# A graph network kernel on one core: a second block of 308 edge columns is sorted by source block and takes its rows from X in SBUF by one-hot products

## The chip, the cores and the metric

The kernel runs on one core of a Trainium2 chip. The metric is the device time of one execution in microseconds. Before the change its median is 8972.53 us over 11 runs, which lie between 8945.65 and 8996.13 us. Engines are named as in the profile: PE multiplies matrices (PEld loads its weights), DVE, ACT and POOL do elementwise work, SP issues transfers, and POOL also issues the indirect transfers that gather or scatter rows by an index.

## The reference, cut to what matters

Four graph layers run over one graph of 12500 nodes with 32 features and 400000 edges, which come sorted by destination. Each is followed by a residual sum and a layer norm. The change concerns the third layer, which runs a small network on every edge and takes the largest value at each destination.

```python
src = jax.random.randint(..., (400000,), 0, 12500)
dst = (12500 * jax.random.uniform(..., (400000,)) ** 2.0)   # then edges are sorted by dst
...
x = _layernorm(x + _L0_gnn_ref(x, src, dst, ...))           # attention over the edges
x = _layernorm(x + _L1_gnn_ref(x, edge_index, 3))           # 3 rounds of neighbour means
x = _layernorm(x + _L2_gnn_ref(x, edge_index, edge_attr_32, ...))
x = _layernorm(x + _L3_gnn_ref(x, edge_index))              # 3 rounds, normalised by degrees

def _L2_gnn_ref(x, edge_index, edge_attr, W1, b1, W2, b2):
    rol, col = (edge_index[0], edge_index[1])
    e_feat = jnp.concatenate([x[rol], x[col], edge_attr], axis=-1)
    h = jax.nn.relu(e_feat @ W1 + b1)
    v = h @ W2 + b2
    x_cand = jax.ops.segment_max(v, col, num_segments=num_nodes)
    return jnp.maximum(x_cand, x[:, -v.shape[-1]:])
```

Because destinations are squared uniforms, many edges share the low destinations.

## The kernel before

**Nodes and edges.** X lies in SBUF as 98 blocks (`H`) of 128 nodes by 32 features. Edges are taken as 3125 columns of 128.

**Stages.** First a matrix A of edge counts is built in DRAM while the attention layer uses it. Then come the three rounds of the second layer (`Rounds.product`, line 370), each a product of X with A. A round walks 25 chunks of 512 destinations; a chunk loads A in two halves (line 352) and runs 98 matmuls for each of its four quarters. Then the edge layer runs, and the three rounds of the fourth layer end the kernel; part of the first of those three is computed inside the edge layer (`round_part`, line 1354), the rest by `product` from block `HS[-1]` on.

**Side work in the second layer's rounds.** `sort_heavy` takes the first 308 columns (`HC`), whose destinations are all below 128, and sorts them by source block into 98 buckets of 512 rows (`sorted_d`). It is cut into steps by generators, and `product` takes a step twice a chunk, 51 in a round. `rank` works in round 0: 28 pieces, each a compare, a scan and a multiply on DVE (lines 606 to 612), four matmuls with `pick` (line 616) and a copy on ACT. `send` works in rounds 1 and 2: each of its 77 steps writes four positions on DVE (line 648) and issues four indirect scatters on POOL (line 116), one for each column; for every 22 columns `rows` loads edge attributes and copies them with two key columns into a row buffer on POOL (lines 636 to 640). Round 2 also scatters 98 blocks of X into `starts_d`, on the same POOL queue. In rounds 1 and 2 DVE also gathers bits of A's tiles (lines 380 to 387).

**The edge layer.** The other 2817 columns are worked in groups of four, in batches of 48 columns (`T`), in three stages of 1984, 512 and 321 columns (cuts by `HS`). For each column POOL issues one gather of source rows from `table` in DRAM (line 111). PE turns the four columns (line 1739), DVE copies the result out of PSUM (`eT`, line 1741), and behind that copy the indices `ids` of the group four ahead are written (line 1717), so gathers run four groups ahead. `hidden` (lines 1770, 1772) and `outer` (line 1788) are the edge network. Per batch DVE runs 64 scans: 32 spread each destination's row over its edges, 32 take running maxima. One stage's results are fetched with gathers when it ends (`done`), and then `round_part` of that stage fills the next.

**The sorted edges in the edge layer.** `heavy` works one bucket of 512 sorted edges as one part, 98 parts in all. Source rows come from a product of `X[:, b, :]` with a one-hot matrix, destination rows from `X[:, 0, :]` with another. A part has 12 steps; `fill` takes two steps at its first call in each group and one at its second, three a group, so 98 parts take 1177 steps or 392 groups, all of them in the first stage. Parts follow each other without overlap, since each holds the one buffer `z` in PSUM from its second step on. After the parts end, groups carry edges alone until a stage has ended.

```python
        def fill(i):
            for _ in range(2 - i):
                next(first[0], None)
            if fillers:
                k = 8 if fillers[0] in begun else 40
```

Tile orders the instructions of each engine when the program is built; the order on each engine is then fixed.

Of the kernel before, what the change touches and what calls it, by code (L numbers as in the profile page):

```python
# [22 lines left out]
P = 128  # L23
D = 32
# [36 lines left out]
HS = (52, 78)  # L61
# [59 lines left out]
def dense_path(ctx, tc, bad_i, x, src, dst, edge_attr, w1T, w1_b, w2, w2T, w2_b, aT,  # L121
# [23 lines left out]
    HE = P * HC  # L145
    ROW = D + 2
    scan = dram.tile([E - HE, D], F32, name="scan")
    sorted_d = dram.tile([H * SLOTS, ROW], F32, name="sorted_d")
# [65 lines left out]
    cuts = [HC]  # L214
# [333 lines left out]
    def sort_heavy(st):  # L548

        keep = st.enter_context(tc.tile_pool(name="h_keep", bufs=1))  # L550
        lo_f = keep.tile([P, HC], F32, name="lo_f")
        d1_f = keep.tile([P, HC], F32, name="d1_f")
        at = []
# [4 lines left out]
        n = HE // NR  # L558
        m = n // 4

        def rank():

            base = keep.tile([P, HC], F32, name="base")
            dsh = hk.tile([P, HC + 1], I32, name="dsh")
            nc.vector.memset(dsh[:, 0:1], -1)
            nc.gpsimd.dma_start(dsh[:, 1:], dst[:HE].rearrange("(p t) -> p t", p=P))
            nc.gpsimd.dma_start(dsh[1:, 0:1], bass.AP(tensor=dst.tensor, offset=dst.offset + HC - 1,
                                                      ap=[[HC, P - 1], [1, 1]]))
            hi = hk.tile([P, HC], I32, name="hi")
            nc.gpsimd.dma_start(hi, src[:HE].rearrange("(p t) -> p t", p=P))  # L570
            yield from range(2)
            nc.vector.tensor_tensor(lo_f, dsh[:, 1:], dsh[:, :HC], op=OP.is_lt)
            bad = hk.tile([P, 1], F32, name="bad")
            nc.vector.reduce_sum(bad, lo_f, axis=AX.X)
            nc.vector.tensor_add(more, more, bad)
            nc.vector.tensor_scalar(bad, dsh[:, HC:], float(P - 1), None, op0=OP.is_gt)
            nc.vector.tensor_add(more, more, bad)
            nc.vector.tensor_scalar(d1_f, dsh[:, 1:], 1.0, None, op0=OP.add)
            lo = hk.tile([P, HC], I32, name="lo")
            nc.vector.tensor_single_scalar(lo, hi, P - 1, op=OP.bitwise_and)  # L580
            nc.vector.tensor_copy(lo_f, lo)
# [3 lines left out]
            nc.scalar.dma_start(hi_d.rearrange("(p t) -> p t", p=P), hi8)  # L585
            nc.vector.tensor_scalar(base, hi, float(SLOTS), SLOTS / 2, op0=OP.mult, op1=OP.add)
            pick = hk.tile([P, 4, 4], BF16, name="pick")
            nc.vector.memset(pick, 0.0)
            for i in range(4):
                nc.vector.memset(pick[:, i, i:i + 1], 1.0)  # L590
# [4 lines left out]
            def load(c):  # L595
                t = hk.tile([P, n], U8, name="hib", bufs=2)
                nc.scalar.dma_start(t[:H], hi_d[None, c * n:(c + 1) * n].to_broadcast([H, n]))
                return t

            late = [load(0)]  # L600
            for c in range(NR):
# [18 lines left out]
                nc.scalar.dma_start(rank_d[c * n:(c + 1) * n].rearrange("(i t) -> i t", i=4), rk[:4])  # L620
            nc.vector.tensor_scalar(carry[:H], carry[:H], float(SLOTS), None, op0=OP.is_gt)
            nc.vector.tensor_add(more[:H], more[:H], carry[:H])
            to = keep.tile([P, HC], F32, name="at")
            nc.scalar.dma_start(to, rank_d.rearrange("(p t) -> p t", p=P))
            yield
            nc.vector.tensor_add(to, to, base)
            at.append(to)

        def send():

            k = HC // 14

            def rows(i):
                t = rp.tile([P, k, ROW], F32, name="hrow")
                u = rp.tile([P, k, D], F32, name="hattr", bufs=1)
                nc.gpsimd.dma_start(u, edge_attr[:HE].rearrange(
                    "(p t) d -> p t d", p=P)[:, i * k:(i + 1) * k, :])
                nc.gpsimd.tensor_copy(t[:, :, :D], u)
                nc.gpsimd.tensor_copy(t[:, :, D], lo_f[:, i * k:(i + 1) * k])
                nc.gpsimd.tensor_copy(t[:, :, D + 1], d1_f[:, i * k:(i + 1) * k])  # L640
                return t

            late = [rows(0)]
            for e in range(0, HC, 4):
                n = min(4, HC - e)
                pos = rp.tile([P, 4], I32, name="pos")[:, :n]
                with tc.issue_after(beats[-1].ins):
                    nc.vector.tensor_scalar(pos, at[0][:, e:e + n], 0.0, float(H * SLOTS - 1),
                                            op0=OP.max, op1=OP.min)
                for j in range(n):  # L650
                    i, u = divmod(e + j, k)
                    if u == 1 and i < 13:
                        late.append(rows(i + 1))
                    put = scatter(nc, sorted_d, pos[:, j:j + 1], late[i][:, u, :])
                    tc.declare_no_dep(put.ins, group="sorted", reason="one row for each edge")
                    tc.add_to_no_dep_group("sorted", put.ins)
                yield

        sent = send()
        return rank(), sent, sent  # L660
# [618 lines left out]
    nc.vector.memset(most, -BIG)  # L1279
    with ExitStack() as st:  # L1280
# [8 lines left out]
        def done(s):  # L1289
# [5 lines left out]
            def finish(h0, k, e):  # L1295
# [3 lines left out]
                if h0 == 0:  # L1299
                    nc.vector.tensor_max(e[:, 0, :], e[:, 0, :], most)  # L1300
                nc.vector.tensor_add(e, e, mb2[:, None, :].to_broadcast([P, k, D]))
# [65 lines left out]

        def fill(i):
            for _ in range(2 - i):
# [13 lines left out]
        def heavy(hidden, outer):  # L1383

            up = hw.tile([P, P], BF16, name="up")
            down = hw.tile([P, P], BF16, name="down")
            one = hw.tile([P, P], BF16, name="one")
            two = hw.tile([P, P], BF16, name="two")
            for t, at, v in ((up, -1.0, 1.0), (down, 1.0, 1.0), (one, 0.0, 1.0), (two, 0.0, 2.0)):
                nc.vector.tensor_scalar(t, jp, at, v, op0=OP.is_equal, op1=OP.mult)  # L1390
            next1 = hw.tile([P, 1], F32, name="next1")
            nc.vector.tensor_scalar_add(next1, place, 1.0)
            col1 = hw.tile([P, P], F32, name="col1")
            nc.gpsimd.iota(col1, pattern=[[1, P]], base=1, channel_multiplier=0,
                           allow_small_or_imprecise_dtypes=True)
            ends = [hw.tile([P, 4, D + 1], F32, name=f"ends{i}") for i in range(2)]
            for t in ends:
                nc.vector.memset(t[:, :, D:], 1.0)

            def load(b):  # L1400
                t = hw.tile([P, 4, ROW], F32, name="hrow", bufs=3)
                nc.scalar.dma_start(t.rearrange("p j d -> p (j d)"),
                                    sorted_d[b * SLOTS:(b + 1) * SLOTS].rearrange(
                                        "(p j) d -> p (j d)", p=P))
# [4 lines left out]

            late = [load(0), load(1)]  # L1410
            yield
            for b in range(H):
                if b + 2 < H:
                    late.append(load(b + 2))
                rw = late.pop(0)
                key = hw.tile([P, 2, 4], BF16, name="key", bufs=2)
                nc.vector.tensor_copy(key, rw[:, :, D:].rearrange("p j k -> p k j"))
                d1 = key[:, 1, :]
                yield
                z = psum.tile([P, CH], F32, name="z")  # L1420
                nc.tensor.matmul(z[:, 0:4], up, d1, start=True, stop=True)
                nc.tensor.matmul(z[:, 4:8], down, d1, start=True, stop=True)
                wide = []
                for m in range(2):
                    y = psum.tile([P, CH], F32, name="y", bufs=2)
                    for j in range(4):
                        nc.tensor.matmul(y[:, j * P:(j + 1) * P],
                                         key[:, m, j:j + 1].to_broadcast([P, P]), one,
                                         start=True, stop=True)
                    wide.append(y)  # L1430
                yield
                hot = hw.tile([P, 2, CH], F32, name="hot")
                nc.vector.tensor_scalar(hot[:, 0], wide[0], place, None, op0=OP.is_equal)
                nc.vector.tensor_scalar(hot[:, 1], wide[1], next1, None, op0=OP.is_equal)
                f = hw.tile([P, 2, 4], F32, name="f", bufs=2)
                kb = hw.tile([P, 4 * D], BF16, name="kb", bufs=2)
                nc.vector.tensor_tensor(f[:, 0], z[:, 4:8], d1, op=OP.is_equal)
# [3 lines left out]
                nc.vector.tensor_tensor(f[:, 1], z[:, 0:4], d1, op=OP.not_equal)  # L1441
                nc.vector.tensor_mul(f[:, 1], f[:, 1], d1)
                yield
                last = hw.tile([P, 4, P], F32, name="last", bufs=2)
                nc.vector.tensor_tensor(last, col1[:, None, :].to_broadcast([P, 4, P]),
# [4 lines left out]
                nc.tensor.matmul(pw[0:D], X[:, b, :], hot[:, 0], start=True, stop=True)  # L1450
                nc.tensor.matmul(pw[D:2 * D], X[:, 0, :], hot[:, 1], start=True, stop=True)
                for j in range(4):
                    nc.tensor.matmul(pT[2 * D:3 * D, j, :], rw[:, j, :D], ident, start=True,
                                     stop=True)
                nc.tensor.matmul(z[:, P:2 * P], kb, two,
                                 start=True, stop=True)
                yield
                eT = hw.tile([3 * D, 4, P], F32, name="heT")
                nc.scalar.copy(eT, pT[:3 * D])
                stay = hw.tile([P, P], F32, name="stay", bufs=2)  # L1460
                nc.scalar.copy(stay, z[:, P:2 * P])
                B = Part()
                B.v = hw.tile([P, 4, D], F32, name="hv", bufs=2)
                yield
                ready = hidden(B, eT)
                yield
                outer(ready)
                yield
                nc.tensor.transpose(z[:, 0:P], B.v.rearrange("p j d -> p (j d)"), ident)
                yield  # L1470
                o = hw.tile([P, P], F32, name="ho", bufs=2)
                nc.vector.tensor_tensor_scan(o, stay, z[:, 0:P], -BIG, OP.min, OP.max)
                yield
                nc.tensor.transpose(z[:, 2 * P:3 * P], o, ident)
                yield
                e = ends[b % 2]
                nc.scalar.copy(e[:, :, :D], z[:, 2 * P:3 * P].rearrange("p (j d) -> p j d", j=4))
                yield
                got = z[:, :4 * (D + 1)].rearrange("p (j d) -> p j d", j=4)
                for j in range(4):  # L1480
                    nc.tensor.matmul(got[:, j, :], last[:, j, :], e[:, j, :], start=True, stop=True)
                yield
                lack = hw.tile([P, 4], F32, name="lack", bufs=2)
# [973 lines left out]
```

## Time and profile before

| what | us |
|---|---|
| median of 11 runs | 8972.53 |
| profiled execution, own time | 8954.37 |
| its span, first to last instruction | 8952.5 |
| second layer, round 0 (1413 to 1900) | 487 |
| second layer, round 1 (1900 to 2490) | 590 |
| second layer, round 2 (2490 to 3130) | 640 |
| edge layer, with sorted parts (3180 to 5740) | 2560 |
| edge layer, edges alone (5740 to 6540) | 800 |
| a round of the fourth layer with no side work (8010 to 8470) | 460 |

A window's row tells the busy time of each engine in a stretch, with the count of its instructions in brackets, then the granted PE clock as a share of full speed, the busy share of the DMA engines and the GB/s moved. A wait's row tells who waited for whom, the sum in us, how often, and the longest. In a group's row the mean of one instruction stands after the busy time, and the idle time before it after the bar. Matmuls of a row overlap, so rows of PE do not add up to PE's busy time. Some matmul records are missing.

### The profile page before, as it was taken

How to read it: one execution, taken by the hardware profiler on the slowest of the kernel's cores; microseconds unless marked ns; L12 is line 12 of the kernel's file. 1: busy time of each engine (PE TensorE's matmuls, PEld its weight loads, DVE VectorE, ACT ScalarE, POOL GpSimd, SP SyncE). 2: the span in 40 equal slices, each digit the busy share in tenths (PEclk: the TensorE clock that was granted, in tenths of full speed). 3: DMA queues.
4: the chain of work that ended last, by engine and by line, in shares of the span. 5: the costliest groups of instructions: out<-in, count | busy, mean ns of one | idle time of the engine just before them, and what ended most of it. 6: DMA issues, size and time to landing. Idle time of an engine off the chain costs nothing. (4 is left out here: it accounts for less than half of the span.)

```text
span 8952.5 us, 194378 instructions
## 1 busy us (share of the span) xinstructions
PE 7030.8 (79%) x84402; PEld 5539.4 (62%) x84402; DVE 3929.0 (44%) x10962; ACT 1632.5 (18%) x3386; POOL 3568.8 (40%) x3459
## 2 busy tenths in 40 slices
PE   6788999998877967777777777656646885889998
PEld 4688998988877834444444444433323553579998
DVE  6999995524433534444444444333333223231111
ACT  1235882000000012112111112111111111100000
POOL 1005110025543155555555555666666556400000
PEclk7889999999988956666566665655557985999999
DMA  1156448988866821111111111111114652679998
GB/s 52 55 223 249 200 202 305 348 321 309 309 244 233 302 68 46 45 39 45 42 46 45 39 45 45 44 44 39 49 40 120 203 173 58 198 247 360 360 356 318
DMA packets 574722, 1447.42 MB, mean 162 GB/s; under 512 B 108407, under 2 KB 269791, under 8 KB 560415
## 3 DMA queue, kind: packets, MB, share of 16 engines
q1 hardware_dynamic: 433200, 1347.10, 41.2%
q0 software_dynamic: 109792, 66.25, 4.4%
q10 hardware_dynamic: 30864, 21.54, 0.9%
q8 instruction: 664, 10.88, 0.5%
q14 instruction: 202, 1.65, 0.1%
HBM read 1155.33 MB, written 279.27 MB: 160 GB/s over the span
## 5 line engine op out<-in xcount | busy, mean ns | idle before, releaser
L111 POOL DMA_INDIRECT ef<-table,ids x2817 | 2667.9, 947 | 1845.0 <-DVE ids L1717 879.7
L370 PE MATMUL y<-x,a 128*128 128x96 bf16 x49980 | 2339.6, 209 | 230.1 <-issue 206.6
L370 PEld LDWEIGHTS <-a 128*128 128x128 fp8e4 x49980 | 2241.3, 100 | 300.0 <-issue 271.4
L1788 PE MATMUL pv<-mw,hT 128*128 128x64 f32 x3208 | 764.0, 381 | 852.8 <-issue 388.7
L1788 PEld LDWEIGHTS pv<-mw,hT 128*128 128x128 f32 x3208 | 645.4, 280 | 1185.4 <-issue 572.5
L1741 DVE COPY eT<-pT 96x512 f32<-96x512 f32 x705 | 478.6, 679 | 1521.4 <-remote 595.5
L1770 PE MATMUL ph<-eT,mw 96*64 96x256 f32 x1410 | 681.3, 580 | 222.2 <-ACT hT L1775 89.2
L1007 PE MATMUL pa<-oh,ol 128*128 128x196 bf16 x4928 | 731.4, 272 | 128.6 <-DVE oh L997 82.0
L1739 PE MATMUL pT<-ident,ef 128*96 128x128 f32 x2817 | 729.1, 367 | 31.2 <-remote 22.9
L1013 ACT ACTIVATE at<-pa 128x784 uint16<-128x784 f32 x816 | 646.8, 824 | 506.9 <-PE pa L1007 477.8
L1775 ACT ACTIVATE hT<-ph,mb 128x256 f32<-128x256 f32 x802 | 380.8, 475 | 1730.0 <-PE ph L1772 607.9
L278 DVE TENSOR_REDUCE v<-y 128x128 f32<-128x384 f32 (+2 forms) x152 | 83.6, 550 | 1372.1 <-PE y L272 802.9
L1772 PE MATMUL ph<-eT,mw 96*64 96x256 f32 x1408 | 681.6, 581 | 0.2 <-issue 0.2
L1739 PEld LDWEIGHTS pT<-ident,ef 128*96 128x96 f32 x2817 | 428.0, 178 | 394.8 <-issue 309.1
L1043 PE MATMUL y<-x,at 128*128 128x102 bf16 x9604 | 639.4, 209 | 10.8 <-DVE x L258 6.3
L116 POOL DMA_INDIRECT sorted_d<-hrow,pos x308 | 410.0, 1331 | 590.9 <-DVE v L1237 221.6
L1007 PEld LDWEIGHTS <-ol 128*128 128x128 bf16 x4928 | 556.9, 149 | 142.8 <-issue 78.9
L997 DVE TENSOR_TENSOR oh<-bins_h,pl 128x1568 bf16<-128x1568 bf16 x616 | 597.3, 970 | 0.0
L1043 PEld LDWEIGHTS <-at 128*128 128x128 fp8e4 x9604 | 556.2, 98 | 24.0 <-issue 11.8
L111 POOL DMA_INDIRECT g<-code_d,ws_i x25 | 216.0, 8639 | 807.3 <-DVE ki L781 588.0
L1354 PE MATMUL y<-a,x 128*96 128x512 fp8e4 (+1 forms) x1950 | 516.2, 402 | 16.2 <-DMA a<-A 8.1
L992 DVE TENSOR_TENSOR ol<-la,lb 128x1024 bf16<-128x1024 bf16 x616 | 422.0, 687 | 64.4 <-PE pa L1007 63.3
(409 smaller groups left out, 7065.3 us busy)
## 6 DMA issues: line engine op xcount, KB each, us to landing
a<-A SPq DMA_DIRECT2D x245, 3136.0 KB
A<-at SPq DMA_DIRECT2D x98, 1568.0 KB
a<-A SPq DMA_DIRECT2D x144, 832.0 KB
ef<-table,ids POOLq DMA_INDIRECT x2817
starts_d<-rows SPq DMA_DIRECT2D x44, 1024.0 KB
attr<-in_edge_attr SPq DMA_DIRECT2D x57, 768.0 KB
begin<-starts_d SPq DMA_DIRECT2D x57, 768.0 KB
scan<-o SPq DMA_DIRECT2D x57, 768.0 KB
```

Source lines behind the costliest of these rows:

```text
L111: return nc.gpsimd.indirect_dma_start(out=o, out_offset=None, in_=tab, in_offset=IndirectOffsetOnAxis(ap=idx, axis=0))
L370: nc.tensor.matmul(y[:, q, :], block(h, q - q0), x3[:, h, :3 * F], start=(q + h == first), stop=(c >= CX and q == nq - 1 and h == H - 1))
L997: nc.vector.tensor_tensor(oh, bins_h[:, None].to_broadcast([P, 4, HJ, 2]), pairs(pl[:, t, 0, half * 64 + w0:half * 64 + w0 + 8])[:, :, Non ...
L1007: nc.tensor.matmul(pa[:, 2 * b + i, :HJ], ols[t][:, :, :, 4 * u + 2 * b + i].rearrange("p a b -> p (a b)"), ohs[t][:, 2 * u + b, :, i], st ...
L1013: nc.scalar.activation(at[:, qd, :, off:off + 8].rearrange("p h (w j) -> p h w j", w=4), pa[:, :, :HJ].rearrange("p w (h j) -> p h w j", h ...
L1043: nc.tensor.matmul(y[0][:, q, :], at[:, q - 2 * half, h, :], x3[:, h, :3 * F0], start=(q + h == 0), stop=(not EARLY <= c < CX and last and ...
L1354: nc.tensor.matmul(y[:3 * D, :nq * Q], x3[:, h, :3 * D], a[:, :nq, h - h0, :], start=(h == lo), stop=(h == hi - 1))
L1739: nc.tensor.transpose(pT[:3 * D, j, :], B.ef[:, t + j, :], ident)
L1741: behind = nc.vector.tensor_copy(eT[:, :k], pT[:3 * D, :k])
L1770: nc.tensor.matmul(ph[:HID, :ka], mw1, eT[:, :ka], start=True, stop=True)
L1772: nc.tensor.matmul(ph[HID:2 * HID, :k - 2], mw1, eT[:, 2:k], start=True, stop=True)
L1788: nc.tensor.matmul(pv[:, j].rearrange("p h d -> p (h d)"), hT[:, j, :], mw2, start=True, stop=True)
```

## The change

The columns 308 to 615, whose destinations must lie below 512, are ranked, sent and worked like the first 308. `sorted_d` doubles in buckets and gains a column for the destination block (its rows grow from 34 to 35 words). The edge layer keeps 2509 columns. `HS` moves from (52, 78) to (56, 82), so that its stages have 1764, 492 and 253 columns, and `T` from 48 to 44. In round 0 the two ranks run one after the other, two steps at a time. `send` has 88 steps of seven columns, and its row buffers hold 14 columns.

`heavy` now has 196 parts, of kind 0 (as before) and kind 1 by turns. A kind 1 part takes its four possible destination blocks at once: one product with `X[:, 0:4, :]`, from which a comparison with the block number selects (`sel`), a hidden layer in four matmuls with the weights split in two, and a last product that is 132 wide, for four blocks, instead of 33. A part is cut into `front` (6 steps for kind 0, 8 for kind 1) and `back` (5 steps); the back of one part is worked along with the front of the next. `fill` takes 7 steps in two groups instead of 6. The last products of all parts go into `most` (block 0) and `most4` (blocks 0 to 3).

```diff
-HS = (52, 78)
+HS = (56, 82)
...
+        def ranks():
+            for g in range(2):
+                steps = rank(g)
+                for _ in steps:
+                    next(steps, None)
+                    yield
...
-            k = HC // 14
+            k = 14
...
             late = [rows(0)]
-            for e in range(0, HC, 4):
+            for e in range(0, 2 * HC, 7):
...
-                for j in range(n):
+                for j in range(7):
...
         def fill(i):
-            for _ in range(2 - i):
+            turn.append(i)
+            for _ in range(1 if len(turn) % 4 == 0 else 2):
                 next(first[0], None)
...
+            def hidden4(B, eT, sel):
+                ph = psum.tile([P, 2, P], F32, name="ph")
+                for o, sl in ((ph[:HID], slice(0, 2)), (ph[HID:], slice(2, 4))):
+                    nc.tensor.matmul(o, w_sa, eT[:2 * D, sl], start=True, stop=False)
+                    nc.tensor.matmul(o, w_d, sel[:, sl], start=False, stop=True)
+                hT = hw.tile([P, 2, P], F32, name="hhT")
+                nc.scalar.activation(hT, ph, AF.Relu, bias=mb1)
+                return B, 0, 4, hT
...
+                if kind:
+                    y = psum.tile([P, CH], F32, name="y", bufs=2)
+                    nc.tensor.matmul(y, X[:, 0:NB, :].rearrange("p h d -> p (h d)"), hot[:, 1],
+                                     start=True, stop=True)
+                    yield
+                    sel = hw.tile([P, 4, P], F32, name="sel")
+                    nc.vector.scalar_tensor_tensor(sel.rearrange("p j e -> p (j e)"), wb, blk, y,
+                                                   op0=OP.is_equal, op1=OP.mult)
...
+                for j in range(4):
+                    nc.tensor.matmul((pT if j % 2 else z)[:, j // 2 * W4:(j // 2 + 1) * W4],
+                                     B.last[:, j, :],
+                                     e4[:, j].rearrange("p b d -> p (b d)"), start=True, stop=True)
...
+            for i in range(2 * H):
+                B = Part()
+                B.i, B.b, B.kind = i, i // 2, i % 2
+                for _ in front(B):
+                    next(prev, None)
+                    yield
+                for _ in prev:
+                    yield
+                prev = back(B)
...
-    T = 48
+    T = 44
```

## Prediction

> **What bounds the kernel now.** I read the slices first, then a table of windows by stage, then the waits and the timeline inside the stages that the change touches. The product rounds come first in time. In the table, the figures after each engine are its busy time and, in brackets, its instructions; the last three are granted PE clock, DMA share and GB/s.
>
> ```profile
> 1413.00:1900.00 487.00, 468.26 (x10263) 448.97 (x10264) 198.33 (x265) 26.74 (x77) 0.13 (x1) 0.99 0.96 353
> 1900.00:2490.00 590.00, 509.95 (x10311) 486.55 (x10308) 259.81 (x455) 15.43 (x52) 321.11 (x242) 0.92 0.82 304
> 2490.00:2880.00 390.00, 297.40 (x5252) 274.96 (x5250) 137.25 (x232) 3.31 (x15) 161.41 (x159) 0.82 0.61 225
> 2880.00:3130.00 250.00, 227.97 (x4826) 220.91 (x4823) 128.66 (x199) 2.46 (x12) 46.10 (x48) 0.94 0.83 309
> 8010.00:8470.00 460.00, 446.40 (x10176) 443.33 (x10175) 53.85 (x164) 14.92 (x50) 0.00 (x0) 0.99 0.96 363
> ```
>
> The reader is to see that a round without POOL work does 10176 matmuls in 460 us, 45.2 ns each, and that the same matmuls take longer as soon as POOL (fifth figure) scatters. At 45.2 ns the second, third and fourth windows would take 466, 237 and 218 us; they take 124, 153 and 32 us more. The same windows asked for the scatters alone hold 204, 148 and 48 of them: 0.61, 1.03 and 0.67 us lost for each. The timeline shows how:
>
> ```profile
> 2620.40 0.96 POOL L116 DMA_INDIRECT sorted_d<-hrow,pos  x1 [0.30 <-issue]
> ...
> 2621.66 0.96 POOL L116 DMA_INDIRECT starts_d<-X,start_i  x1 [0.30 <-issue]
> 2622.22 0.37 PE L370 MATMUL y<-x,a 128*128 128x96 bf16 x5 [1.04 <-issue]
> ...
> 2622.93 0.96 POOL L116 DMA_INDIRECT starts_d<-X,start_i  x1 [0.30 <-issue]
> ...
> 2623.67 0.41 PE L370 MATMUL y<-x,a 128*128 128x96 bf16 x3 [1.07 <-issue]
> ```
>
> While scatters follow each other every 1.26 us, PE does three to five matmuls and then stands for about 1 us, waiting for nothing that the profile shows.
>
> The edge layer is the other half:
>
> ```profile
> 3180.00:5740.00 2560.00, 1868.71 (x8574) 1153.87 (x8573) 1056.77 (x4155) 509.11 (x1320) 1466.97 (x1551) 0.60 0.18 43
> 5740.00:6540.00 800.00, 480.68 (x1667) 254.74 (x1667) 261.25 (x1041) 117.52 (x298) 508.44 (x538) 0.51 0.19 46
> 6780.00:7330.00 550.00, 458.40 (x2394) 271.22 (x2392) 173.73 (x693) 90.56 (x238) 323.49 (x342) 0.89 0.60 185
> ```
>
> and of the waits between 3100 and 5700 us, who waited for whom, sum, times, longest:
>
> ```profile
> POOL ef L111 <- DVE ids L1717: 561.5, 162, 8.3
> POOL ef L111 <- issue: 416.9, 1319, 2.2
> ```
>
> First the sorted parts run (1551 POOL instructions, nearly all gathers), then edges alone, then edges with the fourth layer's product. Four gathers, one group, take 2560/1551 x 4 = 6.60 us, 800/538 x 4 = 5.95 us and 550/342 x 4 = 6.43 us. POOL itself needs 4 x (0.95 + 0.30) = 5.0 us. The rest it waits for `ids`, which DVE writes behind the copy `eT`, which waits for PE. So PE's chain sets the pace, not POOL. A group costs PE 4.82, 3.57 and 5.36 us of busy time; times the granted clock (0.60, 0.51, 0.89) this is 2.89, 1.82 and 4.77 us of full-speed work, and PE stands idle 1.78, 2.38 and 1.07 us a group.
>
> **What is removed.** 2817 columns are 705 groups, 2509 are 628. The sorted parts take 1177/3 = 392 groups before; after, a pair takes 6 + 8 = 14 steps, 98 x 14 / 3.5 = 392 groups. So the 77 groups saved are ones without parts: 55 in the first stage (496 to 441) at 5.95 us, 327 us, and 22 in the later two at 6.43, 141 us. Against the 141 stand 100 more matmuls of `round_part` (82 rows for 78, 25 chunks) at 516.2/1950 = 0.265 us, 26 us, and a tail: the last stage has 64 groups, its product begins about 27 groups in and needs 26 x 25 / 16 = 41, so four groups' worth, 64 x 0.265 = 17 us, is left over. Together **-425**. Batches go from 60 to 59 and not to 53, since `T` shrinks: some 5.6 batches of 64 scans at 0.295 us, 106 us of DVE, are not saved. DVE is a third busy there, which hides most; without that cover all of it: 0 to 106, I take **+20**. The later rest of the fourth layer's first round starts from block 82 instead of 78: 400 of 2000 matmuls less in the 120 us from 7880, **-24**.
>
> **Round 0.** A second rank is 28 more pieces. On DVE 28 x 5.9 us (0.94 + 3.15 + 0.15 + 1.62) = 165 us more beside 198 busy of 487: hidden by the waits for PE, and if that cover failed PE would wait for the post-processing. On PE the four matmuls of line 616 took 22.7 us for 112, and PE has no room in this window. ACT copies and its transfers (28 loads and 28 stores more on ACT's queue, 27 us busy of 487) are off the path. 10 to 60, **+25**.
>
> **Rounds 1 and 2.** 308 more scatters, in 51 + 37 steps of seven, so 14 a chunk instead of 8. Queued behind them on POOL are the 98 scatters to `starts_d`; behind the wait for a free `pos` on DVE stand the reductions and with them the PSUM buffers of PE. Row loads go from 14 to 44. Ends: 0.61 us each, the cheapest row, where DVE's long bit operations hold POOL (a scatter then takes up to 7.85 us and PE does not stutter), 188 us; or POOL itself as the bound, 308 x 1.27 + 30 row loads x 4.5 us (copies 0.78 + 0.22 + 0.22, issue 0.58, wait 2.67) = 526. The densest window, 1.03, is nearest for both rounds, but about three of fourteen will fall under bit operations: 0.9 x 308 = **+277**.
>
> [...]
>
> **The sorted parts.** The first kind comes at the same rate (0.25 a group for 0.255). New is 0.25 of a kind 1 part. The trace gives kind 0 in full-speed PE work: (2.89 - 1.82)/0.255 = 4.2 us. Kind 1 by the rows, in busy us a part: kind 0 sums to 8.3 (wide 1.04; the three overlapping products and turns 2.35 in the timeline; 0.29; shifts 0.36; hidden 0.82; outer 0.95; turns 0.82; last 1.69). Kind 1 has 12 wide matmuls for 8 (1.56), one small product with the turns (1.9), a full one (1.9), 0.29, shifts in float32 twice 0.36, hidden twice 0.82, 0.95, 0.82, and the last one 132 wide, which the trace lacks: 1.69 if weights bound it, 6.8 if columns do, 8 x 0.38 = 3.06 by the 128-wide turn of line 1469. Sum 12.8, 1.54 times kind 0. Work a group: 1.82 + 0.25 x 4.2 x 2.54 = 4.5 us.
>
> What a group then takes is work over clock plus idle. Low end: as beside the fourth layer's product, whose work is 4.77: 6.43 us, -66 us over 392 groups. High end: clock and idle as now, 4.5/0.60 + 1.78 = 9.28, +1050. The product in the low row waits for nobody, while the parts chain PE to DVE and ACT through one `pv` and one `ph` in PSUM; yet busier PE was granted more clock in these rows. I take the middle of both, clock 0.75 and idle 1.42: 4.5/0.75 + 1.42 = 7.42, 0.82 x 392 = **+321**. DVE gets about 1.8 us a group more (two compares 1.48, `last` and `sel` 1.32, eight more at 0.28 to 0.74, a quarter of 7.3) on 2.72: 61% of 7.42, not the bound. ACT stays under 35%.
>
> [...]
>
> Zeroing grows by about 2 MB beside a build whose DMA share is 0.57 to 0.65 (600 to 1500 us): 0.
>
> **The sum.** -425 + 20 - 24 + 25 + 277 + 321 = +194. On the profiled execution's own 8954.4 us (span 8952.5 and 1.9 around it) that is 9148; it lies 18 below the median of the runs, so for the median 8972.5 + 194 = **9167**.
>
> **Rivals.**
> 1. *PE absorbs the second kind* (faster). Place: the groups with parts. The clock rises as beside the product and a group stays at 6.60: the 321 go, -127, **8845**. It decides below 6.60 + 127/392 = 6.92 us a group. For it: the product's window. Against: the kind there now already costs 0.65 us a group. 0.26.
> 2. *POOL becomes the bound of rounds 1 and 2.* The send takes 526 instead of 277: +443, **9415**. For it: `pos` already waits for scatters' landing; against: POOL is busy 321 of 590 us. 0.13.
> 3. *The clock stays at 0.60.* +1050 instead of 321: +923, **9895**. For it: 0.51 to 0.60 wherever PE waits for others; against: 0.89 at 83% busy. 0.09.
> 4. *It doesn't do what it says*: a bucket over 512 rows, or a destination over 511, sends the input down the general path. 39424/98 = 402 edges a bucket and 12500 x (78848/400000)^2 = 486 speak against: 0.01. Effects that cancel within 0.2%, about what this kernel's runs can tell from no change: 0.04.
>
> **How the numbers follow.** My forecast has 0.47, own range 8990 to 9400. Slower is 0.47 + 0.13 + 0.09 + 0.01 = 0.70, faster 0.26, same 0.04. The range 8800 to 9600 leaves out rival 3 and a third of rival 1, about 0.18.
>
> **What would show it.** Rounds 1 and 2 together near 1500 us for 1230, with more "issue" waits before line 370; POOL near full there if rival 2 holds. Groups with parts at 7.4 us, clock near 0.75; under 6.9 proves me wrong and rival 1 right. 2509 gathers; 5.95 us still where edges run alone. Round 0 near 510. I am wrong altogether if scatters in longer runs cost less than 0.6 us and groups stay at 6.6.

## The result, and the profile after

The changed kernel takes 9618.46 us (median of 8 runs, 9577.71 to 9641.01) against 8972.57 (31 runs): a ratio of 1.0714, interval 1.0698 to 1.073. It is slower, as forecast, but by 646 us where 194 were predicted, and 18 us outside the range of 8800 to 9600. The profiled execution, from which all stages below are read, took 9562.93 us; its span is 609 us longer than that of the kernel before.

The stages of the profiled execution, by the same windows as before (busy time and instructions of PE, PEld, DVE, ACT and POOL, then granted PE clock, DMA share, GB/s). First the three rounds of the second layer, then the edge layer with sorted parts, with edges alone, and with the fourth layer's product:

```profile
1475.00:2016.00 541.00, 459.10 (x9638) 423.57 (x9639) 344.69 (x368) 37.71 (x101) 0.13 (x1) 0.98 0.82 297
2016.00:2773.00 757.00, 569.25 (x10237) 519.79 (x10234) 256.61 (x433) 15.42 (x52) 493.89 (x484) 0.84 0.67 241
2773.00:3605.00 832.00, 597.44 (x10221) 541.27 (x10218) 276.69 (x456) 5.98 (x28) 421.35 (x436) 0.79 0.56 205
...
3633.00:6768.00 3135.00, 2526.26 (x13672) 1583.24 (x13673) 1668.36 (x6441) 785.13 (x2121) 1509.43 (x1572) 0.76 0.15 38
6790.00:7130.00 340.00, 169.44 (x668) 102.48 (x666) 115.64 (x494) 47.61 (x122) 214.94 (x229) 0.51 0.19 47
7560.00:8010.00 450.00, 399.38 (x2103) 238.12 (x2102) 152.04 (x652) 74.61 (x194) 265.64 (x281) 0.92 0.64 204
```

The fourth row is the largest loss: 392 groups in 3135 us are 8.00 us each, where 6.59 stood before. Edges alone still take 340/229 x 4 = 5.94 us. The copies `eT` and the reductions that end the blocks of a round give the stages of every kernel in the same way; the table below holds them. Round 0 is counted here from the end of its first block to that of its last (443 us before, where the prediction's window had 487), and rounds 1 and 2 from there. A group with parts is the mean of the first 392; "groups after" runs from copy 392 to the last copy (in brackets, how many), "tail" from there to the end. Each row is one profiled execution.

| kernel | round 0 | rounds 1+2 | us a group with parts | groups after | tail | span |
|---|---|---|---|---|---|---|
| before | 443 | 1235 | 6.59 | 2042 (313) | 1153 | 8952.5 |
| after | 541 | 1589 | 8.00 | 1585 (236) | 1207 | 9561.1 |
| b0, kernel before again | 445 | 964 | 5.00 | 1705 (313) | 1152 | 7715.4 |
| a0, changed kernel again | 541 | 1377 | 5.92 | 1299 (236) | 1222 | 8260.0 |
| e1 one block sent | 545 | 1122 | 5.96 | 1296 | 1211 | 8008.0 |
| e2 kind 1 idle | 542 | 1411 | 5.16 | 1305 | 1216 | 7991.8 |
| e3b ranks spread | 521 | 1382 | 5.94 | 1296 | 1215 | 8235.6 |
| e4 plain transfers | 541 | 1309 | 5.95 | 1298 | 1212 | 8185.1 |
| e5 more PE work | 544 | 1383 | 5.93 | 1304 | 1211 | 8258.5 |
| e6 more DVE work | 544 | 1376 | 7.42 | 1296 | 1216 | 8833.1 |
| e7 HS back | 541 | 1372 | 5.91 | 1302 | 1155 | 8180.3 |
| e8 gathers 8 ahead | 544 | 1387 | 5.98 | 1271 | 1245 | 8277.8 |
| e9 positions ahead | 550 | 1340 | 5.94 | 1300 | 1209 | 8215.1 |
| e10 e9, e3b, e7, e8 | 526 | 1396 | 5.89 | 1267 | 1188 | 8181.9 |
| e11 e9, start values ahead | 552 | 1086 | 5.96 | 1299 | 1214 | 7982.2 |
| e12 eT on ACT | 540 | 1377 | 5.42 | 1291 | 1210 | 8026.1 |
| e13 e11, e3b, e7, e12 | 525 | 1151 | 5.42 | 1303 | 1156 | 7746.1 |
| e17 e9, start values first | 550 | 967 | 5.91 | 1297 | 1222 | 7846.6 |
| e16 e17, e3b, e7, e12 | 527 | 968 | 5.43 | 1302 | 1166 | 7586.9 |
| e15 kernel before, eT on ACT | 441 | 962 | 5.00 | 1693 (313) | 1154 | 7698.3 |

All the experiments ran on five chips on which the kernel before takes 7707 to 7729 us, and not 8972; so they are compared with b0 and a0, the two kernels unchanged on one such chip, and not with the first two rows. Most experiments are a single execution; e13, e15 and e16 have 6, 10 and 5 runs. Stages that an edit does not touch differ by up to 34 us in rounds 1 and 2 (1411 in e2, 1377 in a0) and by under 0.1 us a group.

There the change costs 545 us of span for 609, and partly by other waits. Who waited for whom in rounds 1 and 2 (1904 to 3139, 2016 to 3605, 1908 to 2872 and 2016 to 3394 us), sum, times, longest. PE in the kernel before, then PE and DVE in the changed kernel, all in the first pair:

```profile
PE y L370 <- issue: 165.0, 318, 1.4
```

```profile
PE y L372 <- issue: 364.3, 633, 1.9
```

```profile
DVE pos L677 <- DMA sorted_d<-hrow,pos: 123.6, 16, 10.5
```

The same for PE in b0, then PE and DVE in a0:

```profile
PE y L370 <- issue: 45.4, 75, 2.0
```

```profile
PE y L274 <- DVE spread L267: 188.2, 19, 13.5
PE y L372 <- DMA a<-A: 137.6, 13, 19.8
...
PE y L372 <- issue: 13.7, 24, 1.2
```

```profile
DVE pos L677 <- DMA sorted_d<-hrow,pos: 747.2, 81, 12.7
```

So the stops without a wait that the prediction priced rose from 165.0 to 364.3 us in the first pair, and hardly occur in a0. What holds PE in a0 is named: DVE stands 747 us before the next seven positions, because the scatters that read the last but one set have not landed; the copies into `spread` (line 267) and the reading of A's tiles stand behind it on DVE, and PE waits for `spread` and for the next tiles of A.

### The profile page after: what moved, and what is told of

The parts are those of the page before. It is cut to its first block, busy times and chain, and to the rows that moved or that the text cites. A ratio compares the mean times of both kernels' runs of the same rounds, so it can differ in the third digit from the quotient of the medians.

```text
span 9561.1 us, 205071 instructions
## 1 busy us (share of the span) xinstructions
PE 7599.0 (79%) x88296; PEld 5923.8 (62%) x88296; DVE 4566.0 (48%) x12909; ACT 1850.2 (19%) x4039; POOL 3690.4 (39%) x3626
## 5 line engine op out<-in xcount | busy, mean ns | idle before, releaser
L111 POOL DMA_INDIRECT ef<-table,ids x2509 | 2400.7, 957 | 2193.7 <-DVE ids L1859 981.0
L372 PE MATMUL y<-x,a 128*128 128x96 bf16 x49588 | 2449.5, 212 | 415.4 <-issue 392.3
L372 PEld LDWEIGHTS <-a 128*128 128x128 fp8e4 x49588 | 2303.4, 101 | 538.8 <-issue 509.3
L116 POOL DMA_INDIRECT sorted_d<-hrow,pos x616 | 735.7, 1194 | 523.0 <-issue 185.8
L1930 PEld LDWEIGHTS pv<-mw,hT 128*128 128x128 f32 x2900 | 513.1, 248 | 664.4 <-issue 298.3
L1930 PE MATMUL pv<-mw,hT 128*128 128x64 f32 x2900 | 608.0, 345 | 316.4 <-ACT hT L1917 135.7
L1912 PE MATMUL ph<-eT,mw 96*64 96x256 f32 x1256 | 547.0, 528 | 205.9 <-DVE eT L1883 123.1
L1881 PE MATMUL pT<-ident,ef 128*96 128x128 f32 x2509 | 525.7, 335 | 37.5 <-remote 16.4
L1914 PE MATMUL ph<-eT,mw 96*64 96x256 f32 x1254 | 554.9, 535 | 0.1
L1529 PE MATMUL pT<-hot,X 128*32 128x512 f32 x392 | 319.6, 912 | 259.2 <-DVE hot L1508 256.6
L1881 PEld LDWEIGHTS pT<-ident,ef 128*96 128x96 f32 x2509 | 343.8, 157 | 239.2 <-issue 183.3
```

The source lines that it names most:

```text
L111: return nc.gpsimd.indirect_dma_start(out=o, out_offset=None, in_=tab, in_offset=IndirectOffsetOnAxis(ap=idx, axis=0))
L116: return nc.gpsimd.indirect_dma_start(out=tab, in_=i, in_offset=None, out_offset=IndirectOffsetOnAxis(ap=idx, axis=0))
L372: nc.tensor.matmul(y[:, q, :], block(h, q - q0), x3[:, h, :3 * F], start=(q + h == first), stop=(c >= CX and q == nq - 1 and h == H - 1))
L1881: nc.tensor.transpose(pT[:3 * D, j, :], B.ef[:, t + j, :], ident)
L1912: nc.tensor.matmul(ph[:HID, :ka], mw1, eT[:, :ka], start=True, stop=True)
L1914: nc.tensor.matmul(ph[HID:2 * HID, :k - 2], mw1, eT[:, 2:k], start=True, stop=True)
```

## The experiments

**The two kernels again (b0, a0).** No edit.

> The kernel before, unchanged, to have its stages in this chip's clock beside the others of this set. If this chip grants more PE clock than in the profile of before (the first four experiments had 5.95 us a group with both kinds of parts), then a group with parts takes 5.0 to 5.4 us for 6.59 and one without 4.9 to 5.2 for 5.95; if the clock is the old one, all stages are as they were within 2%.

> The changed kernel, unchanged, beside the kernel before in the same set. Theory: three terms carry the loss (scatters in rounds 1 and 2, the second kind's work, round 0), of which the scatters' does not depend on the granted clock: rounds 1 and 2 stay 150 us or more over before's, round 0 70 to 100 us over, groups with parts 0.6 us or more over. Rival: all of the loss comes from the low granted clock; then at a higher clock the kernels are within 2% of each other.

The windows with parts of b0 and of a0:

```profile
2897.00:4859.00 1962.00, 1628.59 (x8685) 1013.51 (x8685) 1062.81 (x4206) 510.68 (x1333) 1485.54 (x1565) 0.72 0.24 58
```

```profile
3417.00:5739.00 2322.00, 2046.43 (x13682) 1317.06 (x13683) 1654.40 (x6443) 785.42 (x2121) 1509.74 (x1574) 0.95 0.21 52
```

The rival is out: with more clock the loss stays, +96 in round 0, +413 in rounds 1 and 2, 0.92 us a group (+360). In b0 a group with parts takes 5.00 us, which is POOL's 4 x (0.95 + 0.30), a gather and the wait before the next (1485.54/1565 and 358.3/1176 us), and PE waits 280.8 us for gathered rows: there the gathers set the pace, and not PE's chain as in the profile that was read for the prediction.

**One block sent (e1), plain transfers (e4).**

```diff
-            for e in range(0, 2 * HC, 7):
+            for e in range(0, HC, 7):
```

> Leaves out the second block's row loads and 308 scatters (its buckets stay zero); all else is as in the changed kernel. Theory: rounds 1 and 2 grew from 587+649 to 774+834 us because of the scatters, about 1.2 us each; without them the two rounds take 1230 to 1270 us together and the kernel about 9240 us. Rival: they grew for another reason (seven scatters to a step in place of four, or PE's own pace on this program); then the rounds stay over 1450 us together.

```diff
-                    put = scatter(nc, sorted_d, pos[:, j:j + 1], late[i][:, u, :])
+                    if g:
+                        r0 = (c0 + j) * P
+                        put = nc.scalar.dma_start(spare_d[r0:r0 + P], late[i][:, u, :])
+                    else:
+                        put = scatter(nc, sorted_d, pos[:, j:j + 1], late[i][:, u, :])
```

> The second block's 308 scatters become plain transfers of the same 128 rows of 140 bytes to a spare place in DRAM, issued from ACT; its buckets stay zero. Theory: what stops PE beside a scatter is POOL's indirect transfer and its descriptors; then rounds 1 and 2 take 1240 to 1330 us together. Rival: the many small writes themselves hold up PE's loads of A or its instructions; then they stay at 1500 to 1610 us.

Both leave the second block's buckets empty. Without its scatters the rounds fall by 255 us to 1122. They stay 158 above b0 with the same 308 scatters. At seven to a step these all fall into the first of the two rounds, where DVE still waits 334.9 us for positions (83.5 in both rounds of b0); the second round takes 469 us. So it is not the number of scatters alone. e4 met its figure (1309) and still settled nothing: DVE waited 335.7 us for positions of the first block, and the transfers put on ACT's queue held ACT's casts of X for 103 us. It moved a queue rather than took it away.

**Positions ahead (e9, e11, e17).** The positions of a block are written once at the end of its rank.

```diff
-                    nc.vector.tensor_scalar(pos, at[g][:, c0:c0 + 7], 0.0,
-                                            float(2 * H * SLOTS - 1), op0=OP.max, op1=OP.min)
+                pos = at[g][:, c0:c0 + 7]
...
+            nc.vector.tensor_scalar(at[g], to, 0.0, float(2 * H * SLOTS - 1), op0=OP.max,
+                                    op1=OP.min)
```

> The scatter positions of a whole block are written once, at the end of its rank in round 0, in place of seven at a time on DVE (line 677) between the scatters. Where PE does not stop without a wait (the two chips of the first eight experiments), theory: rounds 1 and 2 grew from 964 to 1377 us because DVE stood 671 us in front of line 677, waiting for scatters to land, with PE's reductions queued behind; without that wait they take 970 to 1100 us. Rival: the scatters hold PE and the loads of A directly; then they stay over 1300 us. On a chip as slow as that of the prediction's profile, PE's stops without a wait remain and the two rounds stay over 1450 us.

The theory's figure is missed: 1340 us lie in the rival's range, over 1300. But the cause is not the rival's. The wait of DVE for positions was gone, and another had come, in the first of the two rounds (2013 to 2887; the second takes 466 us), DVE then PE:

```profile
DVE run L541 <- POOL run L528: 421.9, 2, 278.7
PEld L274 <- DVE spread L267: 258.1, 1, 258.1
PE y L274 <- DVE spread L267: 258.0, 1, 258.0
```

With nothing to hold them, the scatters fill POOL's queue. Three small values, one word for each partition, that the index preparation takes from POOL (line 528) come among them: some 300 scatters are issued between the first value and the last. DVE stands for 422 us in two waits, and PE for 258 us behind one of them. So these values must come first:

```diff
-                nc.gpsimd.iota(run, pattern=[[0, 1]], base=P * cuts[s] - HE - 1,
-                               channel_multiplier=Cs, allow_small_or_imprecise_dtypes=True)
...
+        nc.gpsimd.iota(run0[s], pattern=[[0, 1]], base=P * cuts[s] - HE - 1,
+                       channel_multiplier=cuts[s + 1] - cuts[s],
+                       allow_small_or_imprecise_dtypes=True)
```

> As the run with positions written ahead, and the three start values of the index preparation (POOL, line 528) are written before the sends instead of among them, so that DVE does not wait for POOL to come through its queue of scatters. Theory: scatters cost rounds 1 and 2 their 413 us only through what waits for them in the queues of DVE and POOL; with both waits gone the two rounds take 930 to 1030 us (964 in the kernel before) and the kernel is 340 to 440 us below the changed one. Rival: the scatters take PE's time or the bandwidth of A's loads directly; then the rounds stay over 1150 us.

> As the run before with positions and start values ahead, but the start values are made at the start of the kernel: in that run they still came behind the first scatters and DVE waited 139 us for them once. Theory: rounds 1 and 2 go from 1086 to 940 to 990 us, so that 616 scatters cost no more than the 308 of the kernel before (964). Rival: 120 us of direct cost remain, 1060 to 1100 us.

In e11 the values were still issued behind the first scatters, and DVE waited for them once, 138.6 us; the rounds took 1086 us, between the two forecasts. In e17 they are made where the kernel begins. Its two rounds:

```profile
2021.00:2515.00 494.00, 456.85 (x10258) 450.34 (x10258) 256.86 (x380) 15.41 (x52) 399.70 (x362) 0.99 0.98 365
2515.00:2988.00 473.00, 446.82 (x10202) 440.99 (x10200) 268.25 (x416) 5.96 (x28) 337.06 (x284) 1.00 0.95 354
```

967 us with 616 scatters, 964 in b0 with 308; PE stops without a wait for 50.1 us, 45.4 in b0. So on this chip the 308 added scatters themselves cost the product 3 us; the rest of the 413 us was waiting, for positions in a0 and, once these were written ahead, for the start values. POOL is busy 81% and 71% and is not the bound.

**The second rank (e3b).**

```diff
-                    next(steps, None)
+                    turns.append(0)
+                    if len(turns) % 2:
+                        next(steps, None)
```

> The two ranks take two, then one step by turns (76 steps in the 51 calls of round 0) in place of two at every call. Theory: two steps at one call put two rank pieces on PE's path close together, and PE waits for DVE's one mask buffer; spread out, round 0 falls from 514 to about 470 to 490 us and PE's wait for the mask from 74 to under 35 us. Rival: the doubled amount of rank work costs it, however it is spread; then round 0 stays at 505 to 520 us.

A miss: 521 us, at the edge of the rival's range. The forecast started from 514 us where the table has 541, so the fall that it named, 24 to 44 us, came to 20. PE's wait for the mask falls, here in the changed kernel of the result and in e3b, but not under 35:

```profile
PE pr L636 <- DVE one L632: 73.9, 45, 2.2
```

```profile
PE pr L636 <- DVE one L632: 48.2, 26, 2.2
```

PE's busy time in round 0 grows from 426.66 in b0 to 460.03 in a0; these 33 us and a0's wait for the mask, 73 us, cover the +96.

**What sets a group with parts (e2, e5, e6, e8, e12).** e2 leaves out the kind 1 parts and puts empty turns in their place; e5 does its last four matmuls three times (`for j in 3 * list(range(4))`); e6 does `sel` five times (`for _ in range(5)`); e8 sets `AHEAD = 8`; e12 moves the copy:

```diff
-            behind = nc.vector.tensor_copy(eT[:, :k], pT[:3 * D, :k])
+            behind = nc.scalar.copy(eT[:, :k], pT[:3 * D, :k])
...
-            nc.vector.tensor_copy(ids[:, :k], rows[:, e:e + k])
+            nc.scalar.copy(ids[:, :k], rows[:, e:e + k])
```

> Leaves out all work of the kind 1 parts in the edge layer, with their steps kept as empty turns, so a pair of parts still takes 14 steps. Theory: the second kind's own work raised a group from 6.6 to 8.0 us; without it a group is at 6.4 to 6.7 us over the first 392 groups, PE clock 0.60 to 0.65, and the kernel about 9040 to 9100 us. Rival: the new order (the back of one part beside the front of the next, seven steps in two groups) makes the groups long; then a group stays over 7.2 us.

> The four last matmuls of a kind 1 part are done three times over (same result): 8 more matmuls of 132 columns, 3.4 us of PE a part at 0.42 us each, 0.84 us a group. Theory: PE's own work sets a group's time; then groups with parts get longer by 0.5 to 0.9 us (200 to 350 us in all). Rival: what sets it is the waiting from engine to engine, or POOL; then they get longer by less than 0.3 us.

> The selection on DVE (line 1549) is done five times over: 2.97 us of DVE a part more, 0.74 us a group. Theory (PE's own work sets a group's time, DVE has room): groups get longer by less than 0.25 us. Rival (PE and DVE work by turns in a fixed order, so that time on either lengthens a group): by 0.4 to 0.75 us.

> Gathers run eight groups ahead in place of four (AHEAD). Theory: with parts, groups come unevenly, PE keeps up with five us a group on average, and POOL's waits for indices (0.7 us a group) come from the unevenness; then a group with parts falls from 5.92 to 5.0 to 5.5 us. Rival: the chain of PE and DVE through a pair of parts is as long as its 3.5 groups; then a group stays at 5.8 to 6.0 us.

> The copy of each group's turned rows out of PSUM (eT) and the writing of the indices behind it move from DVE to ACT: 0.84 us a group off DVE (71% busy with parts) and 0.75 on to ACT (34%). Theory: with parts, DVE's place in the chain sets a group's time (five selections for one made a group 1.5 us longer, eight more matmuls nothing); then a group falls from 5.92 to 5.0 to 5.5 us. Rival: the order of steps on PE sets it; then it stays at 5.7 to 6.0 us.

Their windows with parts, in the order e2, e5, e6, e12:

```profile
3448.00:5471.00 2023.00, 1771.32 (x8706) 1072.78 (x8705) 1104.50 (x4397) 527.18 (x1440) 1529.55 (x1567) 0.68 0.23 56
```

```profile
3420.00:5744.00 2324.00, 2150.64 (x15231) 1450.42 (x15231) 1656.95 (x6443) 776.57 (x2121) 1515.70 (x1574) 0.98 0.22 52
```

```profile
3413.00:6321.00 2908.00, 2538.46 (x13681) 1572.58 (x13681) 1929.39 (x6835) 780.94 (x2123) 1499.51 (x1575) 0.78 0.17 42
```

```profile
3402.00:5525.00 2123.00, 1989.70 (x13676) 1254.35 (x13675) 1390.39 (x5657) 1008.67 (x2905) 1532.65 (x1574) 0.99 0.22 57
```

The second kind is the price: without its work a group is at 5.16 us, close to the 5.00 of POOL's gathers. That does not free the new order of the charge, since in e2 no back of a part has another part's front beside it. More PE work costs next to nothing: 8 more matmuls a part, 1549 instructions more in the window, cost 2 us in all. PE's clock went from 0.95 to 0.98 and its idle time from 276 to 173 us, and together these took them in. More work on DVE cost twice itself: 392 more selections of 0.74 us are 290 us, and the window grew by 586, beyond both forecasts. PE waits for `sel`,

```profile
PE ph L1465 <- DVE sel L1550: 165.6, 98, 2.2
```

which a0 does not have, and its clock falls, from 0.95 to 0.78, so that PE's own busy time goes from 2046 to 2538 us for the same matmuls; only 94 of the 586 us are more idle time. Taking 0.84 us a group off DVE (e12) gains 0.50, at clock 0.99; whether by DVE's lighter load or because the copy no longer stands behind the parts' work in DVE's order, e12 does not tell. Gathers eight ahead (e8) change nothing with parts (5.98), take 28 us off the groups after and lengthen the tail by 23. So on these chips DVE's place in the chain sets the time of a group, at 71% busy (1654 of 2322 us).

**HS back (e7).** `HS = (52, 78)`.

> HS goes back to (52, 78): the stages have 1676, 512 and 321 columns. Theory: the tail grew because the last stage is too short to hide its product; from the last edges to the fourth layer's first block goes back from 166 to 85 to 100 us, the direct product after it grows by 17 to 20 us, so the kernel gains 40 to 70 us. Rival: the two cancel with longer groups in the last stages; then the change is under 15 us.

The tail falls from 1222 to 1155 us and the groups stay. The theory holds; the whole kernel gains 80 us, a little over its bound.

**Together (e10, e13, e16), and the control (e15).**

> All four edits at once (positions written ahead, ranks spread evenly, eight groups ahead, HS back). If the causes are separate, the gains add up: round 0 -20, rounds 1 and 2 -280 to -400, groups with parts -160 to -360, tail -40 to -70, so 500 to 850 us below the changed kernel, and at the time of the kernel before or up to 300 us below. Rival: the gains overlap or are refused, and it stays over 2% slower than before.

> Positions and start values ahead, ranks spread evenly, HS back to (52, 78), and eT on ACT together. Theory (the terms are separate): rounds 1 and 2 at 930 to 1030 us, round 0 at 510 to 530, groups with parts at 5.0 to 5.5 us, tail -67, so 7450 to 7750 us, at or below the kernel before. Rival: eT on ACT does nothing or costs; then 7750 to 7900 us.

> All edits that helped, with the start values at the kernel's start. Theory: rounds 1 and 2 at 940 to 990, groups with parts at 5.3 to 5.4 us, tail -67: 7520 to 7640 us, 1 to 2.5% below the kernel before. Rival: something else waits for POOL's queue next; then 7680 to 7760 us.

> The kernel before, with eT and the indices on ACT as in the best version, to see whether that edit alone helps without the change. Theory: there POOL's gathers set the pace (5.00 us a group with parts, 4 x 1.25), so the kernel stays within 1% of itself. Rival: DVE's load holds it as well, and it gains over 1%.

e10 still holds e9's wait for POOL (rounds 1 and 2 at 1396 us); it gains 78 us and stays 6% slower than before, so the theory's sum fails. e13 gives 7744.49 us, ratio 1.0037 (1.0024 to 1.005): its total is in the forecast, its rounds 1 and 2 (1151 us) are not, with one wait of 202.2 us left for a start value. e16 gives 7588.7 us, ratio **0.9839** (0.9825 to 0.9852) to the kernel before: 1.6% faster, in the forecast. Its window with parts:

```profile
2991.00:5118.00 2127.00, 1994.40 (x13673) 1258.85 (x13673) 1389.45 (x5653) 1008.93 (x2905) 1534.39 (x1574) 0.99 0.23 57
```

e15 stays at 0.9984 (0.9974 to 0.9993): eT on ACT is worth little where POOL's gathers set the pace; its 5.00 us a group did not move. So of e16's gain nearly all is the second block, freed of its waits: 403 us fewer in the groups after (1705 to 1302) pay for 82 in round 0 and 165 with parts. It takes eT on ACT for that: with a0's 5.92 us a group in place of 5.43 the parts would cost 192 us more, an estimate, and the block would not pay.

## Why the prediction was too low

Its terms against the table, in the first pair of profiles. The 17 us of leftover product, which the prediction has within its -425, are put to the tail, where they fall:

| term | predicted | measured |
|---|---|---|
| round 0 | +25 | +98 |
| rounds 1 and 2 | +277 | +354 |
| groups with parts | +321 | +553 |
| saved groups, scans | -422 | -457 |
| tail, with leftover product | -7 | +54 |
| sum (with 7 us between stages) | +194 | +609 |

The median moved by 646 and not 609 us because the profiled execution of the changed kernel was 56 us below its median, that of the kernel before 18 below.

**Parts: the step that failed most (+232).** The prediction wrote a group as PE's full-speed work over clock plus idle, 4.5/0.75 + 1.42 = 7.42. Measured, it is 4.90/0.76 + 1.55 = 8.00 (work 2526.26 x 0.76/392, idle (3135 - 2526.26)/392). Clock and idle were near; the mis-sized term of this sum is the work, 0.40 us too low, which is 0.53 of the missing 0.58 us at the forecast clock. A kind 1 part came to about (4.90 - 1.82)/0.25 - 4.2 = 8.1 us of full-speed work, an estimate with the prediction's own 1.82 and 4.2, where it expected 1.54 x 4.2 = 6.5.

But such a sum always adds up, since a window is busy time plus idle time; it does not say what sets the time. The step that failed there is "DVE gets about 1.8 us a group more ... 61% of 7.42, not the bound". On the chip of a0, e5 adds about 0.42 us a group of full-speed PE work (2150.64 x 0.98 less 2046.43 x 0.95, over 392) and the group stays at 5.93 us, while e6 and e12 show that time on DVE is what a group pays for. A low busy share was read as room, though PE waits on DVE several times in each part; the share was 53% in the result's profile (1668.36 of 3135 us). There too the wait of PE with the largest sum is one for DVE, between 3633 and 6768 us:

```profile
PE pT L1529 <- DVE hot L1508: 256.6, 95, 4.0
```

No edit was run where the kernel before takes 8972 us, so that DVE sets a group's time there too is argued and not shown. Of the 1.41 us that a group grew by, 0.92 appear in a0 as well; the other 0.49 come only in the first pair.

**Rounds 1 and 2 (+77).** "0.9 x 308" priced a scatter by the stops of PE. It came to 354/308 = 1.15 us, over the densest window of before. In the first pair the place was right and the size off: the stops at the product grew by 199 us (165.0 to 364.3), those on all lines of PE by 227, and PE's busy time for the same matmuls by 128 (1038 to 1167) at a lower clock (0.89 to 0.81). That a scatter must cost PE something is wrong elsewhere, as e17 shows. The text had named the other wait, DVE behind `pos`, and gave it no price; in a0 that wait is what the scatters cost. Rival 2, POOL as the bound, did not happen: POOL was busy 494 of 757 us in the first of the two rounds and 421 of 832 in the second.

**Round 0 (+73).** The cover, "hidden by the waits for PE", covered DVE's work but not PE's wait for it: two rank steps at one call need the one mask buffer twice, and PE waits 73.9 us. The second rank's PE work itself was within the term's 10 to 60 us (33 us more PE time in a0 than in b0). e3b gives only 20 us of the 96 back.

**Tail (+61).** "Four groups' worth" of leftover product, 17 us, was 78: from the last copy to the end of the fourth layer's first block it takes 166 us for 88 before. e7 gives back 67 us of the tail. The rest of it fell by 24 us, as forecast. The saved groups were worth 35 us more than forecast.

The first rival (PE absorbs the second kind) had its mechanism partly right: in e5 PE's clock rises from 0.95 to 0.98 and, with 102 us less idle time, absorbs the PE work. It failed on DVE's part in the chain. The third (the clock stays at 0.60) did not happen: 0.76.

Two things stay open. Why PE stops and is granted less clock in the first pair of profiles than in the others was not found: between 3180 and 5740 us of the kernel before PE waits 204.3 us at line 1788 for nothing that the profile shows, in b0 not at all.

```profile
PE pv L1788 <- issue: 204.3, 127, 7.9
```

And none of the edits was tried where the kernel before takes 8972 us; that e16 beats it is shown on one chip alone, where the kernel before takes 7717 us.

## What to carry to other kernels

Before a transfer is added, look at what refills its operands: in a0 an index tile of two buffers, written by a busy engine between scatters, turned the landing time of the scatters into 747 us of waiting on DVE, with what was queued behind that write held too; write indices well ahead, then look at what else now stands behind the longer queue (in e9 start values, 422 us). Price added work by which engine the others wait for, not by busy shares. To find that engine, do the suspected work several times over, on one engine at a time, as e5 and e6 do. And count with PE's clock: here 290 us added on DVE, for which PE waits, cost 586 us (e6, clock from 0.95 to 0.78), and 1549 instructions added on PE cost 2 us (e5, clock from 0.95 to 0.98).

## What the runs showed of the hardware

At the same matmuls PE's granted clock was lower where PE stood idle longer in the stretch with parts: 0.78 with 370 us idle of 2908 (e6), 0.95 with 276 of 2322 (a0) and 0.99 with 133 of 2123 (e12). Among PE's largest waits there the longest single one is 2.2 us in e6, where PE waits 98 times for `sel`, 165.6 us in all; it is 1.2 us in a0 and 0.9 us in e12. The size shown is that 290 us of added DVE work became 586 us.

The kernel before took 8972 us in the runs of the result and 7707 to 7729 us on the five chips of the experiments. Its rounds without side work ran at almost the same rate (10176 matmuls in 460 us in the first profile, 10037 in 450 us in b0, at clocks of 0.99 and 1.00); its groups with parts did not (6.59 and 5.00 us each, at clocks of 0.60 and 0.72).
